# Pairwise outer products with batch norm: other pieces for the stores of rows 38 to 31, and the last sample stored through GpSimd's queue

## The chip, the core and the metric

The kernel runs on one core of one Trainium2 chip. The metric is the device time of one execution in microseconds. A core has five engines with an instruction stream each: TensorE (PE in the profile), VectorE (DVE), ScalarE (ACT), GpSimd (POOL) and SyncE (SP). Data moves between the device's memory and the on-chip memory (128 partitions) by 16 DMA engines; a transfer is issued by an instruction of SP, ACT or POOL into a queue of that engine, and every queue is worked off by the same 16 DMA engines.

## What is computed

For 1024 samples there are two inputs of 39 features with 16 numbers each. For every pair of features (r, c) with c < r, 741 pairs in all, the kernel forms the 16 x 16 outer product of one feature of `xj` and one of `xi`, normalises it by the mean and variance of that pair over the whole batch, and multiplies it by a 16 x 16 weight:

```python
_ROWS, _COLS = np.tril_indices(F1, k=-1)          # 741 pairs, F1 = 39
cross = xj[:, rows, :, None] * xi[:, cols, None, :]
mean = jnp.mean(cross, axis=(0, 2, 3), keepdims=True)
var = jnp.mean(jnp.square(cross - mean), axis=(0, 2, 3), keepdims=True)
normed = (cross - mean) * jax.lax.rsqrt(var + BN_EPS)
normed = normed * gamma[None, :, None, None] + beta[None, :, None, None]
out = normed[:, :, None, :, :] * W[None, None, :, :, :]
return jnp.transpose(out, (0, 2, 1, 3, 4))
```

The output has the shape (1024, 1, 741, 16, 16) in float32: 777 MB, against 6 MB that are read.

## The kernel before

**Tiles.** A partition holds 8 samples (`NT = 8`), so 128 partitions hold all 1024. A *row* r is the set of its r pairs (r, 0) to (r, r-1). One tile is one row for two neighbouring samples (`T = 2`) of every partition, so each row has four tiles, for t0 = 0, 2, 4, 6. The list `tiles` (lines 69 to 76) starts with row 19 (four tiles), then row 20 and its partner 18 in turns, then row 38 (four tiles, no partner), then 37 with its partner 1, 36 with 2, and so on down to 21 with 17. A row and its partner have 38 pairs together; they share a half of the big buffer `y_sb`, and the two halves are used in turns. So a tile writes to the place of the tile two such pairs earlier, and its first instructions have to wait until the stores of that earlier tile have read it. The very last tile of the list is row 17 with t0 = 6.

**The work of one tile.** A batch statistic is folded into a scale and a shift for each pair beforehand (lines 301 to 507). Then, tile by tile (loop at line 523):

- `scale_xi` (POOL, line 169) multiplies the features of `xi` by the scale of each pair, two tiles ahead.
- `products` (lines 177 to 203) makes the outer products: one instruction per sample t and per i of 16, each over all r pairs of a row. In rows above 33 ScalarE does 11 of 16 and GpSimd 5 (`POOL_I_LONG`); else 12 and 4 (`POOL_I`). Sample 0's come first, then sample 1's. Rows up to 4 are done on VectorE (line 192).
- `finish` (lines 254 to 299) adds the shift and multiplies by the weight, pair by pair and for both samples at once: `stt` on VectorE (line 291). A share of the pairs goes to GpSimd: in rows above 33 (`LONG`) eight pairs just ahead of the middle, p0 to p1 with p1 = r // 2, for which ScalarE adds the shift (line 275) and GpSimd multiplies by the weight in two lots of four (line 280); in the other rows 13% of the pairs, at the end of the row, with the shift on GpSimd too (line 277). ScalarE's additions for one tile come ahead of the next tile's products in its stream.
- After each piece that `bounds` names, `finish` calls `store`.

**Pieces and stores.** `bounds(n)` cuts the pairs of a tile into pieces. The first eight tiles have hand-written ones; of the others, rows above 30 (`ONE`) have two equal pieces, the rest one. `store` (lines 205 to 219) issues on SP's queue. In a tile from number 8 on (`whole`) of a row above 19 it stores sample 0 piece by piece and sample 1 as a whole, when the last piece is done. So row 38 has three stores per tile: pairs 0 to 18 of sample 0, pairs 19 to 37 of sample 0, and all 38 pairs of sample 1. Rows 30 to 20 have two, one per sample. A partner row (up to 19) goes out in one store with both samples.

SP works through its stores in order; each waits for the engines that made its piece. Everything is scheduled by hand (`manual_schedule`): the order in which the instructions are written is each engine's order.

Of the kernel before, what the change touches and what calls it, by code (L numbers as in the profile page):

```python
# [14 lines left out]
T = 2  # L15

ONE, LONG = 30, 33
FIRST_PIECES = (  # L20
    (0, 1, 3, 6, 10, 14, 19), (0, 4, 9, 14, 19), (0, 4, 11, 19), (0, 9, 19), (0, 10, 20), (0, 9, 18), (0, 10, 20), (0, 9, 18)
)
# [18 lines left out]
def tile_pair_outer_batchnorm(  # L41
# [15 lines left out]
    nc = tc.nc  # L57
    P = nc.NUM_PARTITIONS
    NB, F, E = xi.shape
    NT = NB // P  # L60
    EE = E * E
# [7 lines left out]
    tiles = [(mid, t0, t0 // T * half // 2) for t0 in range(0, NT, T)]  # L69
# [25 lines left out]
    out_v = out.rearrange("(p t) o n i j -> p t (o n i j)", t=NT)  # L95
# [41 lines left out]
    def view(n):  # L137
        r, _, u = tiles[n]
        return y_sb[:, u : u + T * r, :].rearrange("p (t n) e -> p t n e", t=T)
# [65 lines left out]
    def store(n, c0, c1, t_from=0, t_to=T):  # L205
        r, t0, _ = tiles[n]
        n0 = first[r]

        whole = n >= len(FIRST_PIECES)
        step = 1 if r > mid and (whole or c1 == r) else t_to - t_from  # L210
        for t in range(t_from, t_to, step):
            if whole and step == 1 and t == t_to - 1:
                if c1 < r:
                    continue
                c0 = 0
            nc.sync.dma_start(  # L216
                out_v[:, t0 + t : t0 + t + step, (n0 + c0) * EE : (n0 + c1) * EE],
                view(n)[:, t : t + step, c0:c1, :].rearrange("p t n e -> p t (n e)"),
            )
# [14 lines left out]
    def weigh(n):  # L234

        y = view(n)
        for c0, c1 in zip(bounds(n), bounds(n)[1:]):
            affine(n, range(c0, min(c1, OWN)), (nc.vector,))
            nc.vector.tensor_tensor(  # L239
                y[:, :, c0:c1, :],  # L240
                y[:, :, c0:c1, :],
                w_dve.unsqueeze(1).to_broadcast([P, T, c1 - c0, EE]),
                ALU.mult,
            )
            store(n, c0, c1)

    def bounds(n):
        if n < len(FIRST_PIECES):
            return FIRST_PIECES[n]
        r = tiles[n][0]  # L250
        pieces = 1 + (r > ONE)
        return tuple(q * r // pieces for q in range(pieces + 1))

    def finish(n):

# [32 lines left out]
        for t in range(0, T, size):  # L288
            for c0, c1 in zip(bounds(n), bounds(n)[1:]):
                for c in [*range(c0, min(c1, p0)), *range(max(c0, p1), c1)]:  # L290
                    stt(  # L291
                        y[:, t : t + size, c, :],
                        y[:, t : t + size, c, :],
                        t_sb[:, n0 + c : n0 + c + 1],
                        w_dve.to_broadcast([P, size, EE]),
                        ALU.add,
                        ALU.mult,
                    )
                store(n, c0, c1, t, t + size)
# [262 lines left out]
```

## Time and profile before

| what | value |
|---|---|
| median of 4 runs | 1879.22 us (1879.03 to 1879.45) |
| the profiled execution's own time | 1879.06 us |
| its span, first to last instruction | 1877.3 us |
| VectorE busy | 1723.7 us (92%), 2640 instructions |
| ScalarE busy | 1645.8 us (88%), 3416 instructions |
| GpSimd busy | 1532.3 us (82%), 1746 instructions |
| TensorE busy | 26.0 us (1%) |
| read from, written to the device's memory | 6.00 MB, 776.99 MB |
| one pair on VectorE for two samples (line 291) | 737 ns on average (a little below 0.66 us without a gap in the rows looked at) |
| ScalarE waits for stores in its products (line 147) | 150.4 us, 81 times, longest 4.4 us |

The profile is that of one execution. "Busy" leaves out waiting, and instructions that only issue a transfer. The page gives the span in 40 slices of 47 us with the busy share in tenths (9 is 90% or more) and what the DMA engines moved in GB/s. It also lists groups of instructions by line, with the tile that they write on the left of the arrow and the tiles that they read on the right. In a line of the timeline the first two numbers are the start and the length of a run of instructions in us, then come engine, line, operation, tiles, shapes and the count; in brackets stands how long the engine had been idle before it and what ended that. A trace also holds a record of each DMA packet, with its queue, start, length and size; which of the 16 DMA engines moved it isn't recorded, but packets of one engine follow each other without a gap of more than some ns, so that they can be chained.

### The profile page before, as it was taken

To read this page: it belongs to the slowest core of one execution; us is meant where nothing else is said; L and a number is where in the kernel's file an instruction comes from. 1 tells how busy PE (TensorE), PEld (TensorE's weight loads), DVE (VectorE), ACT (ScalarE), POOL (GpSimd) and SP (SyncE) were. 2 spreads that over 40 slices of the span, in tenths; PEclk is the share of its full clock that TensorE was granted. 3 is DMA by queue.
4 is the path that set the end of the run, shared out by engine and by line. 5 is a ranking of instruction groups with operands and counts; after the bars stand their busy time and mean duration, and the time that the engine had idled before them with its cause. 6 is when DMAs were issued, how large, how long until landed. Compare 5 with 4: busy or idle time off the path is not lost.

```text
span 1877.3 us, 9638 instructions
## 1 busy us (share of the span) xinstructions
PE 26.0 (1%) x130; PEld 23.3 (1%) x130; DVE 1723.7 (92%) x2640; ACT 1645.8 (88%) x3416; POOL 1532.3 (82%) x1746
## 2 busy tenths in 40 slices
PE   4000000000000000000000000000000000000000
PEld 4000000000000000000000000000000000000000
DVE  8999888899999999999999999999999999999994
ACT  8999888888888899989999999998999998989892
POOL 8999778787777788888888888888888888888882
DMA  5999999999999999999999999999999999999998
GB/s 200 386 420 424 411 423 420 429 425 424 428 426 425 428 426 426 427 425 427 419 425 432 425 425 432 425 432 423 431 425 430 425 431 426 429 428 426 428 429 351
DMA packets 53690, 783.63 MB, mean 417 GB/s; under 512 B 4720, under 2 KB 6384, under 8 KB 17008
## 3 DMA queue, kind: packets, MB, share of 16 engines
q1 hardware_dynamic: 52320, 779.72, 97.9%
q10 hardware_dynamic: 1296, 3.29, 0.5%
q14 instruction: 73, 0.60, 0.1%
q8 instruction: 1, 0.02, 0.0%
HBM read 6.00 MB, written 776.99 MB: 417 GB/s over the span
## 4 chain that ended last, share of the span: by engine, by line
DMA 40%; ACT 12%; DVE 6%; issue 1%; SPq 0%; POOL 0%; ACTq 0%; DVEq 0%; POOLq 0%
DMA out_dram<-y_sb 40%; ACT y_sb L147 12%; DVE y_sb L291 6%; SPq L216 0%; POOL y_sb L277 0%; ACTq L147 0%; DVEq L557 0%; DVEq L291 0%; POOLq L277 0%
## 5 line engine op out<-in xcount | busy, mean ns | idle before, releaser
L291 DVE SCALAR_TENSOR_TENSOR y_sb<-y_sb,st_sb,w_dve 128x512 f32<-128x512 f32 (+1 forms) x2511 | 1653.1, 737 | 117.4 <-issue 104.0
L147 ACT ACTIVATE y_sb<-xs,xj_sb 128x288 f32<-128x288 f32 (+20 forms) x3194 | 1514.8, 567 | 181.3 <-DMA out_dram<-y_sb 150.4
L149 POOL TENSOR_SCALAR y_sb<-xs,xj_sb 128x480 f32<-128x480 f32 (+27 forms) x1126 | 604.7, 561 | 14.1 <-DMA out_dram<-y_sb 14.0
L280 POOL TENSOR_TENSOR y_sb<-y_sb,w_sb 128x2048 f32<-128x2048 f32 (+3 forms) x155 | 517.7, 3346 | 87.5 <-ACT y_sb L275 77.9
L169 POOL TENSOR_TENSOR xs<-xi_sb,st_sb 128x640 f32<-128x640 f32 (+33 forms) x135 | 183.9, 1362 | 199.9 <-ACT y_sb L147 196.1
L277 POOL TENSOR_SCALAR y_sb<-y_sb,st_sb 128x512 f32<-128x512 f32 x291 | 196.8, 692 | 5.1 <-ACT y_sb L147 5.1
L275 ACT ACTIVATE y_sb<-y_sb,st_sb 128x512 f32<-128x512 f32 x160 | 100.2, 708 | 3.9 <-POOL y_sb L149 2.2
L192 DVE TENSOR_TENSOR y_sb<-xs,ps 128x256 f32<-128x256 f32 (+3 forms) x32 | 24.8, 817 | 0.5
L489 PE MATMUL ps<-y_sb 39*128 39x38 f32 (+37 forms) x76 | 16.4, 397 | 2.8 <-DVE y_sb L475 2.8
L489 PEld LDWEIGHTS ps<-y_sb 39*128 39x128 f32 x76 | 16.3, 329 | 3.1 <-DVE y_sb L475 3.1
L353 ACT ACTIVATE y_sb<-y_sb 128x1248 f32<-128x1248 f32 x8 | 9.9, 1244 | 2.8 <-POOL y_sb L342 2.8
L358 DVE TENSOR_REDUCE y_sb<-y_sb 128x78 f32<-128x1248 f32 x8 | 11.2, 1445 | 0.4 <-ACT y_sb L353 0.4
L147 ACT ACTIVATE y_sb<-xi_sb,xj_sb 128x304 f32<-128x304 f32 x24 | 11.4, 537 | 0.0
L342 POOL TENSOR_TENSOR y_sb<-xi_sb,y_sb 128x1248 f32<-128x1248 f32 x4 | 9.2, 2320 | 2.2 <-ACT y_sb L391 2.2
L239 DVE TENSOR_TENSOR y_sb<-y_sb,w_dve 128x2048 f32<-128x2048 f32 (+4 forms) x6 | 10.7, 1839 | 0.1
L332 DVE TENSOR_REDUCE y_sb<-xi_sb 128x39 f32<-128x624 f32 (+1 forms) x6 | 6.1, 1011 | 3.9 <-DMA xi_sb<-in_r_xi_dram 3.9
L342 POOL TENSOR_TENSOR y_sb<-xj_sb,y_sb 128x1248 f32<-128x1248 f32 x4 | 9.2, 2321 | 0.0
L378 PE MATMUL ps<-y_sb 128*39 128x79 f32 x48 | 8.1, 340 | 15.2 <-DVE y_sb L358 15.0
L232 POOL TENSOR_SCALAR y_sb<-y_sb,st_sb 128x512 f32<-128x512 f32 x8 | 6.4, 813 | 2.1 <-ACT y_sb L147 2.1
L230 ACT ACTIVATE y_sb<-y_sb,st_sb 128x512 f32<-128x512 f32 x9 | 6.5, 805 | 0.2 <-ACT y_sb L147 0.2
L332 DVE TENSOR_REDUCE y_sb<-xj_sb 128x39 f32<-128x624 f32 (+1 forms) x6 | 6.1, 1013 | 0.6 <-DMA xj_sb<-in_r_xj_dram 0.5
L378 PEld LDWEIGHTS ps<-y_sb 128*39 128x39 f32 x48 | 5.8, 177 | 17.2 <-DVE y_sb L358 10.6
(59 smaller groups left out, 37.3 us busy)
## 6 DMA issues: line engine op xcount, KB each, us to landing
out_dram<-y_sb SPq DMA_DIRECT2D x25, 2304.0 KB, 10.4
out_dram<-y_sb SPq DMA_DIRECT2D x12, 3840.0 KB, 21.6
out_dram<-y_sb SPq DMA_DIRECT2D x21, 2048.0 KB, 12.5
out_dram<-y_sb SPq DMA_DIRECT2D x12, 3584.0 KB, 23.1
out_dram<-y_sb SPq DMA_DIRECT2D x12, 3328.0 KB, 24.4
out_dram<-y_sb SPq DMA_DIRECT2D x12, 3072.0 KB, 25.2
out_dram<-y_sb SPq DMA_DIRECT2D x16, 2176.0 KB, 11.0
out_dram<-y_sb SPq DMA_DIRECT2D x8, 4352.0 KB, 24.1
```

Of the source, the lines that this page charges most:

```text
L147: nc.scalar.activation(y, src, AF.Copy, scale=scale)
L149: engine.tensor_scalar(y, src, scale, 1.0, ALU.mult, ALU.mult)
L169: nc.gpsimd.tensor_tensor(xs, xi_sb[:, t0 : t0 + T, 0:r, :], s_sb[:, :, n0 : n0 + r, :].to_broadcast([P, T, r, E]), ALU.mult,)
L192: nc.vector.tensor_tensor(view(n)[:, t].rearrange("p n (i j) -> p n i j", j=E), xs[:, t].unsqueeze(2).to_broadcast([P, r, E, E]), xj_short ...
L275: nc.scalar.activation(y[:, :, c, :], y[:, :, c, :], AF.Identity, bias=t_c)
L277: nc.gpsimd.tensor_scalar(y[:, :, c, :], y[:, :, c, :], t_c, 1.0, ALU.add, ALU.mult)
L280: nc.gpsimd.tensor_tensor(y[:, :, c0:c1, :], y[:, :, c0:c1, :], w_sb.unsqueeze(1).to_broadcast([P, T, c1 - c0, EE]), ALU.mult,)
L291: stt(y[:, t : t + size, c, :], y[:, t : t + size, c, :], t_sb[:, n0 + c : n0 + c + 1], w_dve.to_broadcast([P, size, EE]), ALU.add, ALU.mult,)
L332: nc.vector.tensor_reduce(total[:, t0:t1, part(x)], sources[x][:, t0:t1], AX.X, ALU.add)
L342: nc.gpsimd.tensor_tensor(devs[n % 7], sources[x][:, t0 : t0 + T], shift[:, x : x + 1, :].unsqueeze(3).to_broadcast([P, T, F, E]), ALU.sub ...
L378: nc.tensor.matmul(ps_g[acc][0:F, 0 : 2 * F + 1], lhs, fb[:, t], start=t == 0, stop=t == NT - 1)
L489: nc.tensor.matmul(ps[:, :, first[r] - n0 : first[r] - n0 + r], pick[:, r, :], stq[:, :, 0:r], start=True, stop=True,)
```

## The change

Three edits. `bounds` gives rows 36 to 31 a first piece of 19, 20, 21, 22, 23, 24 pairs in place of 18, 17, 17, 16, 16, 15; rows 38 and 37 keep 19 and 18. In `store`, `whole` no longer holds for rows 38 and 37, so that their first piece goes out as one store with both samples, and their second piece as one store for each sample: three stores as before, cut differently. And the last tile of all (row 17, t0 = 6), which was one store of both samples on SP's queue, becomes four: sample 0 on SP, then sample 1 as partitions 121 to 125 and 0 to 120 on GpSimd's queue and partitions 126 and 127 on SP's.

```diff
-ONE, LONG = 30, 33
+ONE, LONG, WHOLE = 30, 33, 36
...
     def store(n, c0, c1, t_from=0, t_to=T):
         r, t0, _ = tiles[n]
         n0 = first[r]
-
-        whole = n >= len(FIRST_PIECES)
+        if n == len(tiles) - 1 and t_to - t_from == T:
+
+            store(n, c0, c1, 0, T - 1)
+            for engine, p0, p1 in ((nc.gpsimd, 121, 126), (nc.gpsimd, 0, 121), (nc.sync, 126, P)):
+                engine.dma_start(
+                    out_v[p0:p1, t0 + T - 1, (n0 + c0) * EE : (n0 + c1) * EE],
+                    view(n)[p0:p1, T - 1, c0:c1, :].rearrange("p n e -> p (n e)"),
+                )
+            return
+
+        whole = n >= len(FIRST_PIECES) and r <= WHOLE
         step = 1 if r > mid and (whole or c1 == r) else t_to - t_from
         for t in range(t_from, t_to, step):
             if whole and step == 1 and t == t_to - 1:
...
         if n < len(FIRST_PIECES):
             return FIRST_PIECES[n]
         r = tiles[n][0]
-        pieces = 1 + (r > ONE)
-        return tuple(q * r // pieces for q in range(pieces + 1))
+        if r <= ONE:
+            return 0, r
+
+        return 0, r // 2 + max(0, (WHOLE + 1 - r) * 3 // 2), r
```

## The prediction

> **What bounds the kernel now.** I read the page's slices and DMA queues first.
>
> ```profile
> DMA  5999999999999999999999999999999999999998
> GB/s 200 386 420 424 411 423 420 429 425 424 428 426 425 428 426 426 427 425 427 419 425 432 425 425 432 425 432 423 431 425 430 425 431 426 429 428 426 428 429 351
> q1 hardware_dynamic: 52320, 779.72, 97.9%
> ```
>
> From the second slice on the 16 DMA engines are full; nearly all bytes are stores on SP's queue. 777 MB at about 428 GB/s is 1815 us of the 1877.3 us span. So only three things move the time: stretches in which DMA engines idle, the start, and the end. Slices of 47 us hide such stretches, so next I asked for the busy time in short windows around the rows that change (columns: stretch, length, PE, PEld, DVE, ACT, POOL busy, clock, DMA share, GB/s).
>
> ```profile
> 190.80:193.10 2.30, 0.00 (x0) 0.00 (x0) 1.49 (x3) 2.30 (x5) 0.78 (x2) 1.00 0.00 0
> 239.50:240.30 0.80, 0.00 (x0) 0.00 (x0) 0.00 (x0) 0.80 (x3) 0.00 (x0) 1.00 0.59 243
> 309.70:310.00 0.30, 0.00 (x0) 0.00 (x0) 0.30 (x2) 0.30 (x1) 0.30 (x1) 1.00 0.01 0
> 935.50:936.20 0.70, 0.00 (x0) 0.00 (x0) 0.70 (x2) 0.70 (x3) 0.70 (x2) 1.00 0.30 123
> ```
>
> All engines stand still at 190.8, most or all at 239.5 and 309.7. Chaining the DMA packet records into 16 engines gives the idle time per engine: about 2.35, 0.75 and 0.45 us. At 935.5 (row 30) twelve idle and four work; the same four will matter at the end. The SP timeline shows why 190.8 is empty: the first half of sample 0 of row 38 is issued at 184.13, the rest at 192.32, but the half lasts only 5.8 us (185.05 to 190.85).
>
> ```profile
> 184.13 0.33 SPq L216 DMA_DIRECT2D out_dram<-y_sb  x1
> 192.32 0.81 SPq L216 DMA_DIRECT2D out_dram<-y_sb  x2
> 231.23 0.33 SPq L216 DMA_DIRECT2D out_dram<-y_sb  x1
> 239.40 0.81 SPq L216 DMA_DIRECT2D out_dram<-y_sb  x2
> ```
>
> Next the instruction timeline of the tile two later, (38, t0=4), which reuses that buffer: its 22 products wait for the stores, 11 for sample 0's and 11 for sample 1's, and VectorE waits for the products.
>
> ```profile
> 199.63 7.73 ACT L147 ACTIVATE y_sb<-xs,xj_sb 128x608 f32<-128x608 f32 x11 [0.52 <-DMA out_dram<-y_sb]
> 211.72 7.73 ACT L147 ACTIVATE y_sb<-xs,xj_sb 128x608 f32<-128x608 f32 x11 [4.37 <-DMA out_dram<-y_sb]
> 219.54 19.84 DVE L291 SCALAR_TENSOR_TENSOR y_sb<-y_sb,st_sb,w_dve 128x512 f32<-128x512 f32 x30 [5.92 <-issue]
> ```
>
> Last the DMA view of the end, 1849 to 1877 in 40 slices of 0.7 us.
>
> ```profile
> DMA  9997999989789999989999999982221111100000
> GB/s 474 418 394 332 424 492 461 492 369 430 338 369 471 471 415 490 440 354 459 434 404 404 404 423 448 448 348 100 99 99 75 75 75 75 50 25 25 25 0 0
> ```
>
> One engine moves about 26 GB/s. So at 1868 twelve engines stop, and then four, three, two, one are left: by the packet records they end at 1870.3, 1872.3, 1873.6 and 1876.0, the other twelve at 1867.8 to 1868.2. Queue 14 (instruction fetch) explains it: 62 packets of 8 KB after 27 us, 0.31 us each and some waiting. The four delays, 8.1, 5.6, 4.3 and 2.3 us over the median landing, rank as the instruction counts of ACT (3693), DVE (2935), POOL (2070) and SP (672) do. Each stream seems to be fetched through one DMA engine of its own; TensorE (138) would have a fifth, with next to no delay. The kernel ends when the engine with ACT's fetches is done.
>
> **The change part by part. Rows 38 and 37.** The stores stay three per tile; the first now carries half of both samples. It covers what follows: from 185.05 it lasts 2 x 5.8 = 11.6 us, to 196.65, beyond 192.32 + 0.9 (192.32 to first data at 193.2 is the start of a store). The price: sample 0 now ends as third of four quarters, so its buffer comes free later. Followed through: data of tile (38,0) ends at 202.45 (sample 0) and 208.25 (sample 1) instead of 198.95 and 210.6. The products of (38,4) can start 0.6 after, at 203.05 (3.4 us later than before), run 7.73 to 210.8, then sample 1's to 218.5; the wait of 4.37 is gone, ScalarE itself now sets VectorE's start, 218.6 against 219.54. Its first store is issued 11.7 later (219.54 to 231.23), at 230.3, and could move at 231.2; the queue is full to 208.25 + 4 x 5.8 = 231.45. No idle, 0.25 us to spare. Tile (38,6): products from 226.2, VectorE at 241.7 (242.51 before), data possible at 254.3, queue full to 254.65. Row 37's first tile: VectorE at 264.6 (265.89), data possible at 277.3, queue full to 277.85. Then the margin grows, as products take 7.57 instead of 7.73. So the three stretches go: 2.35 + 0.75 + 0.45 = 3.5 us per engine. On the engine with ACT's fetches it is less, as it lags and idles less in them: some two fetches lie between 185 and 310 (one per 58 us), 0.3 to 0.6 us. I take 2.9. Ends: 3.5, and nothing if ScalarE's start slips by more than the 0.25 us to spare; each us of slip in these tiles comes back as idle.
>
> Does VectorE, while it weighs the second half, have to wait for the two-sample store? No: at 90 to 100 us, where such stores go out piece by piece (ready at 89.23, 93.75, 99.76), it is busy all 10.00 us.
>
> ```profile
> 90.00:100.00 10.00, 0.00 (x0) 0.00 (x0) 10.00 (x16) 10.00 (x23) 9.83 (x13) 1.00 1.00 419
> ```
>
> **Rows 36 to 31.** First pieces grow by 1, 3, 4, 6, 7, 9 pairs. In rows 36 to 34 the piece waits for POOL's share, ready 11.7 us after VectorE's start, while VectorE's 11 to 13 pairs take at most 13 x 0.66 = 8.6: no delay. In rows 33, 32, 31 the first store is issued 6, 7, 9 x 0.66 = 4.0, 4.6, 5.9 us later. What hides it is the queue: bytes issued less bytes moved at that issue are 5.9 to 7.2, 6.5 to 7.0, 7.3 to 8.0 us of work at 428 GB/s. That leaves 1.4 us or more, above the 0.9 of a start. Cost 0. If the lead of 2.9 us were not matched by earlier issues, idle would come back, at most that lead. It is matched: ScalarE waits some 2 us per tile for the previous stores here, so earlier landings start it earlier. Row 30's idle at 935.5 stays; the late engine has none.
>
> **The end.** Before, the last store gives each engine 16 rows of 17 KB (8 partitions, two samples), 0.648 us a row. After, sample 0 still gives 8; sample 1 goes as 5 and 121 partitions on POOL's queue and 2 on SP's. No store of this trace comes from POOL or has such a count. Every store here is split into equal shares of whole rows (128 as 16 x 8). Equal shares of 121 are 11 x 11, of 5 are 5 x 1, and 11 + 5 is 16. So five engines have 1 or 2 rows instead of 8, eleven have 11. If the late engine is one of the five: 6 or 7 rows less, -3.9 or -4.5; take -4.2. If it is one of the eleven: +3 x 0.648 = +1.9. Five streams are fetched and five engines are relieved, so I take the first. The other twelve then end at 1868.1 - 3.5 + 1.9 = 1866.5, before the late one's 1876.0 - 2.9 - 4.2 = 1868.9; a row split small (1 KB packets take 46 ns, 17 of them 0.78 us) adds 11 x 0.13 = 1.5 and stays under it. POOL's issue: between SP's 0.38 us and POOL's longest instruction here, 4.5 us, each; 9 us for both. When it becomes due the queue holds 8.7 us and sample 0 adds 5.2, so it is hidden, and nothing stands behind it on POOL. Two more semaphore waits at the end, 0.06 each: +0.1.
>
> [...]
>
> **Sum.** 1879.06 (this execution; span 1877.3, 1.8 around it; the median shown is 1879.22, 0.16 above) - 2.9 + 0 - 4.2 + 0.1 = 1872.1; I say 1872.0.
>
> **Rivals.** (1) The tail misses: ACT's fetches lie on one of the eleven, or the rows spread evenly. For it: nothing here numbers the engines. Against: the five and five. -2.9 + 1.9 + 0.1 gives 1878.2; spread evenly (0) 1876.3. (2) The middle fails, as the later landing of sample 0 puts ScalarE on the path for more than 0.25 us: only the end gains, 1879.06 - 4.1 = 1875.0. For it the 3.4 us later start, against it the worked margins. (3) Slower: POOL's 121 rows aren't spread. An engine has room until the old end for (1876.0 - (1868.1 - 3.5 - 8 x 0.648)) / 0.648 = 26 rows; from there it decides. 121 has only 1 and 11 as shares, so the price is one engine with 121 rows: 78 us from 1859.4, an end near 1940. Against it: no store in the trace sits on one engine. (4) The change does nothing that counts: the late engine's wait is not what the packets suggest and the removed idle time reappears elsewhere: 1879.
>
> **How the numbers follow.** Forecast 0.56, (1) 0.25, (2) 0.08, (3) 0.06, (4) 0.05. A measurement can tell about 0.2%, 3.8 us: faster means under 1875.5. The forecast and a part of (2) lie there: 0.62; (1), the rest of (2) and (4) but for a little are the same: 0.28; slower 0.10, (3) and part of (1) with a failed middle. Range: below, 3.5 and 4.5 with a little over give 1870.0; above, it takes in (1) at 1878.2: 1878.3.
>
> **What would show it.** Right: no empty window between 185 and 310, (38,4)'s VectorE start near 218.6; a last slice sequence in which no single engine runs on for 8 us, most ending near 1866.5. Wrong: an idle window at first stores of rows 33 to 31; a tail of 25 GB/s as long as before or longer; POOL's packets on few engines.

## The result, and the profile after

The changed kernel takes 1882.34 us (median of 34 runs, 1881.62 to 1883.81) against 1879.19 us (52 runs): the ratio is 1.0018, with a 95% interval of 1.0013 to 1.0023. It is slower by 3.2 us, where 7 us less had been forecast. The profiled execution took 1881.71 us with a span of 1880.0 us.

The page's slices and queues:

```profile
DMA  5999999999999999999999999999999999999998
GB/s 202 386 422 423 426 427 424 426 424 426 427 427 427 426 425 426 429 426 422 425 426 429 426 430 424 431 424 429 429 424 432 428 425 427 431 426 428 426 429 302
q1 hardware_dynamic: 53220, 777.53, 97.7%
q0 software_dynamic: 176, 2.19, 0.4%
```

The fifth slice, with row 38 in it, now moves 426 GB/s (411 before), and the last one 302 (351 before). GpSimd's queue is q0: 2.19 MB and 0.4% of 16 engines' span; its packets took 125 us together by the packet records, where 126 rows of 0.648 us would be 82.

Then the same windows as before the change, moved by 0.3 us because this execution starts a little earlier (columns: stretch, length, PE, PEld, DVE, ACT, POOL busy, clock, DMA share, GB/s):

```profile
190.50:192.80 2.30, 0.00 (x0) 0.00 (x0) 1.53 (x3) 2.30 (x5) 0.82 (x2) 1.00 1.03 440
239.20:240.00 0.80, 0.00 (x0) 0.00 (x0) 0.00 (x0) 0.80 (x2) 0.00 (x0) 1.00 0.93 389
```

The stretch that moved 0 GB/s now moves 440, and the one at 239 moves 389. The SP timeline has the issues as before, 8.2 us apart, but the first one now carries both samples, and its data move until about 196.5 (196.65 had been worked out):

```profile
183.88 0.38 SPq L225 DMA_DIRECT2D out_dram<-y_sb  x1
192.05 1.63 SPq L225 DMA_DIRECT2D out_dram<-y_sb  x2
```

Row 30's idle stretch now stands at 933 and is about half as long (0.39 us per engine on average by the packet records, 0.72 before; the prediction had it stay):

```profile
933.20:933.70 0.50, 0.00 (x0) 0.00 (x0) 0.50 (x2) 0.50 (x2) 0.50 (x2) 1.00 0.29 115
```

Then the timeline of the tile (38, t0=4), whose times had been worked out ahead:

```profile
203.01 15.34 ACT L147 ACTIVATE y_sb<-xs,xj_sb 128x608 f32<-128x608 f32 x22 [4.18 <-DMA out_dram<-y_sb]
218.44 19.84 DVE L302 SCALAR_TENSOR_TENSOR y_sb<-y_sb,st_sb,w_dve 128x512 f32<-128x512 f32 x30 [5.11 <-issue]
226.62 15.35 ACT L147 ACTIVATE y_sb<-xs,xj_sb 128x608 f32<-128x608 f32 x22 [3.17 <-DMA out_dram<-y_sb]
```

The 22 products run without a wait between the samples, from 203.01 (worked out: 203.05), and VectorE starts at 218.44 (218.6); the next tile's products start at 226.62 (226.2). The row part does what the prediction said. So does the lead at the end: sample 0 of the last tile is issued at 1847.88, where the last store was issued at 1850.43 before.

The loss is behind that point. The DMA view of 1846 to 1880 us, in 40 slices of 0.85 us, and the queues in it:

```profile
DMA  9999999999988999699998967776543221100000
GB/s 416 395 421 425 400 405 379 451 395 324 276 219 194 301 296 292 251 424 358 358 271 292 337 184 255 271 276 230 214 164 128 102 123 61 61 20 20 41 0 0
q1 hardware_dynamic: 374, 6.33, 49.7%
q0 software_dynamic: 176, 2.19, 23.0%
out_dram<-y_sb SPq DMA_DIRECT2D x1, 2176.0 KB, 30.6
out_dram<-y_sb POOLq DMA_DIRECT2D x1, 2057.0 KB, 24.2
```

GpSimd's 2 MB took 24.2 us from issue to landing, and sample 0's store on SP 30.6. The timeline of GpSimd shows that its issues were not late, and two windows show what is:

```profile
1848.38 1.28 POOL L212 DMA_DIRECT2D out_dram<-y_sb  x2 [6.75 <-DVE y_sb L302]
```

```profile
1850.00:1852.50 2.50, 0.00 (x0) 0.00 (x0) 0.00 (x0) 0.00 (x0) 0.00 (x0) 1.00 1.00 413
1854.00:1864.00 10.00, 0.00 (x0) 0.00 (x0) 0.00 (x0) 0.00 (x0) 0.00 (x0) 1.00 0.98 291
```

From 1854 on the DMA engines are as busy as before (share 0.98), yet move 291 GB/s instead of 413. GpSimd's first row starts at 1852.77. Busy engines that move less mean that the packets themselves take longer: by the packet records GpSimd's 126 rows of 17 KB took 988 ns on average and up to 3119 ns, where a row of that size took 653 ns (median) before.

Chaining the packet records shows which engine ends last. Four engines lag here as before. In the table a lag is told by the landing of row 17's next to last tile (t0 = 4):

| engine | kernel | lands that tile | rows of 17 KB in the last tile | lost to longer rows | ends |
|---|---|---|---|---|---|
| lags most | rows alone | 1851.67 | 16 | about 0 | 1874.68 |
| lags most | changed | 1850.88 | 8 + 9 = 17 | 1.6 us | 1876.12 |
| lags second | rows alone | 1848.96 | 16 | about 0 | 1872.03 |
| lags second | changed | 1848.36 | 8 + 9 + 1 = 18 | 6.4 us | 1879.10 |

("Rows alone" is the first experiment below. 8 rows are sample 0's on SP's queue, 9 come from GpSimd's queue, 1 from SP's store of two partitions.) So the last engine is no longer the one that lagged most, which is the one with ACT's fetches by the prediction's ranking. The engine that lagged second overtakes it.

### The profile page after: what moved, and what is told of

It reads as the page before. It is cut to its first block, busy times and chain, and to the rows that moved or that the text cites. A ratio compares the mean times of both kernels' runs of the same rounds, so it can differ in the third digit from the quotient of the medians.

```text
span 1880.0 us, 9644 instructions
## 1 busy us (share of the span) xinstructions
PE 26.0 (1%) x130; PEld 23.3 (1%) x130; DVE 1723.7 (92%) x2640; ACT 1645.5 (88%) x3416; POOL 1533.4 (82%) x1748
## 3 DMA queue, kind: packets, MB, share of 16 engines
q0 software_dynamic: 176, 2.19, 0.4%
## 4 chain that ended last, share of the span: by engine, by line
DMA 37%; ACT 13%; DVE 6%; issue 1%; POOL 0%; SPq 0%; ACTq 0%; DVEq 0%; POOLq 0%
DMA out_dram<-y_sb 37%; ACT y_sb L147 13%; DVE y_sb L302 6%; POOL y_sb L288 0%; POOL xs L169 0%; SPq L225 0%; ACTq L147 0%; POOL out_dram L212 0%; DVEq L568 0%; POOLq L568 0%; DVE st_sb L518 0%; DVE ps L511 0%; DVE st_sb L517 0%; DVEq L302 0%; POOLq L212 0%
## 6 DMA issues: line engine op xcount, KB each, us to landing
out_dram<-y_sb SPq DMA_DIRECT2D x16, 2816.0 KB, 24.2
```

## The experiments

Theories at the start: M, two queues at work on the same DMA engines slow each other; S, only the number of rows that each DMA engine gets counts; R, the row changes cost time somewhere. Later P, a row takes longer when an engine reads other partitions than in a store of all 128, and N, a second store at the end costs time, whatever its cut.

**Rows alone, last tile alone, and one store of 128 partitions on another queue.** The first kernel leaves out the special case for the last tile, the second has nothing else. In the third and fourth sample 1 of the last tile is one store:

```diff
-            for engine, p0, p1 in ((nc.gpsimd, 121, 126), (nc.gpsimd, 0, 121), (nc.sync, 126, P)):
+            for engine, p0, p1 in ((nc.gpsimd, 0, P),):      # e4: nc.scalar
```

> The changes to rows 38 to 31 without the change of the last tile. Theory M (two queues at work on the same DMA engines slow each other, so the whole loss lies in the last tile) and theory S (the loss is in how many rows of the last sample each DMA engine gets) both expect 1876.6 us: 1879.2 less the 2.6 us by which the late engine's landings were ahead before the last tile (1853.4 before, 1850.9 after). Theory R (the row changes cost time somewhere) expects 1879 us or more.

> The last tile's change alone, rows as before. M and S: 1879.2 + (1882.3 - 1876.6) = 1884.9 us. R: 1880 us or less.

> As the changed kernel, but sample 1 of the last tile goes in one store of all 128 partitions on GpSimd's queue. S: every engine has its 8 rows again, so 1876.6 us with the end as with one queue. M: rows of two queues still alternate on each engine, the engines move some 280 GB/s instead of 430 while both are live, so 1880 us or more.

> As the changed kernel, but sample 1 of the last tile goes in one store of all 128 partitions on ScalarE's queue. If any second queue slows the engines (M), about the time of the run with GpSimd's queue, 1880 us or more. If the slowing belongs to GpSimd's queue alone (theory G), 1876.6 us. S: 1876.6 us too.

| kernel | us | ratio to before (95%) |
|---|---|---|
| rows alone | 1877.22 | 0.9988 (0.9979 to 0.9997) |
| last tile alone | 1885.55 | 1.0032 (1.0020 to 1.0044) |
| rows, 128 partitions on GpSimd's queue | 1877.48 | 0.9989 (0.9980 to 0.9998) |
| rows, 128 partitions on ScalarE's queue | 1877.16 | 0.9989 (0.9979 to 0.9998) |

The kernel before took 1879.41 us beside them. R falls: the rows alone gain 2.2 us. The last tile alone costs 6.1 us. And M falls: a second queue costs nothing that can be measured, be it GpSimd's or ScalarE's, if the store has all 128 partitions (1877.48 and 1877.16 us against 1877.22). The window of 1854 to 1864 us with GpSimd's 128 rows in it:

```profile
1854.00:1864.00 10.00, 0.00 (x0) 0.00 (x0) 0.00 (x0) 0.00 (x0) 0.00 (x0) 1.00 1.00 426
```

426 GB/s at a share of 1.00, with rows of two queues in turns; GpSimd's 128 rows took 646 to 664 ns each. So it is the cut across the partitions, through the number of rows for each engine (S) or through the length of a row, which S can't explain (988 ns).

**Equal shares, one queue, another cut.** Two stores of 64 partitions on SP's queue give each engine 4 + 4 rows. As a control, two stores of all 128 partitions, of 9 and 8 of the 17 pairs.

```diff
+            for engine, p0, p1 in ((nc.sync, 0, 64), (nc.sync, 64, P)):
...
+            for a, b in ((0, 9), (9, r)):
+                nc.sync.dma_start(
+                    out_v[:, t0 + T - 1, (n0 + a) * EE : (n0 + b) * EE],
+                    view(n)[:, T - 1, a:b, :].rearrange("p n e -> p (n e)"),
+                )
```

> As the changed kernel, but sample 1 of the last tile goes as two stores of 64 partitions on SP's queue: one queue, and 4 + 4 equal rows for each DMA engine. Theory P (a row takes longer when an engine reads partitions other than those that it reads in a store of all 128, since engines then get in each other's way) expects stretched rows, over 0.8 us on average in place of 0.65, and a time of 1879 us or more. Theory S (only the number of rows for each engine counts) expects the time of the kernel with the row changes alone, 1877.2 us, and rows of 0.65 us.

> As the changed kernel, but sample 1 of the last tile goes as two stores of all 128 partitions on SP's queue, 9 and 8 of the 17 pairs. P (the cut across the partitions stretches the rows): rows at the full rate, 1877.2 us. Theory N (a second store at the end costs, whatever its cut): as the two stores of 64 partitions, 1880.6 us.

The halves of the partitions take 1880.57 us (ratio 1.0006, 0.9996 to 1.0016, to a before of 1879.42), the halves of the columns 1877.15 us (0.9991, 0.9982 to 1.0000, to 1879.18). So neither a second store nor GpSimd is needed for a loss of some 3.3 us against the rows alone: the cut across the partitions is enough, at equal shares. Theory S and N fall. The two stretches of 1861 to 1866 us, first the halves of the partitions, then of the columns:

```profile
1861.00:1866.00 5.00, 0.00 (x0) 0.00 (x0) 0.00 (x0) 0.00 (x0) 0.00 (x0) 1.00 1.03 229
```

```profile
1861.00:1866.00 5.00, 0.00 (x0) 0.00 (x0) 0.00 (x0) 0.00 (x0) 0.00 (x0) 1.00 0.91 382
```

All engines are busy in the first, at 229 GB/s, about half of the 426 above. (In the second some are done already, hence 0.91.) The DMA views of 1846 to 1880 us show the whole ends, the rows alone first, then the halves of the partitions:

```profile
DMA  9999999999999899799789823112000000000000
GB/s 411 395 395 446 400 400 430 430 405 405 405 552 388 347 506 445 337 481 496 332 373 594 348 102 143 82 82 102 41 41 41 20 20 0 0 0 0 0 0 0
```

```profile
DMA  9999999999898998999969988966552511000000
GB/s 390 416 420 425 400 425 405 430 405 557 376 470 372 465 465 342 399 312 230 271 189 246 164 246 205 225 164 205 184 164 82 143 61 41 41 20 20 0 0 0
```

With the rows alone twelve engines stop together in slice 24 and the four late ones follow. With the halves the rate falls to 160 to 270 GB/s in slice 19 already, once sample 0's rows run out, and the end is four slices (3.4 us) later.

**GpSimd's two stores by themselves.** They are held back until everything else has landed: GpSimd overwrites one number of sample 0 in each partition of the buffer, which has to wait for SP's store of it (27.22 us of idle time, until 1869.24), and then issues.

```diff
+            nc.gpsimd.memset(view(n)[:, 0, 0:1, 0:1], 0.0)
+            for engine, p0, p1 in ((nc.gpsimd, 0, 121), (nc.gpsimd, 121, 126)):
```

> As the changed kernel, but GpSimd's two stores (121 partitions, then 5) are issued only when sample 0's store has landed: GpSimd first overwrites one number of sample 0 in the buffer, after it was stored. The total is longer by the wait, only the packets count. P: the 121 rows alone, with no second queue, still take well over 0.65 us each, near 1.3 if two engines share; S: 0.65 us. For the shares: 11 rows on eleven engines (as predicted) lasts at least 7.1 us; 8 rows on fifteen engines and one on the last, 5.2 us if unstretched, 10.4 us at 1.3 us a row.

The window of the 121 rows:

```profile
1871.20:1875.20 4.00, 0.00 (x0) 0.00 (x0) 0.00 (x0) 0.00 (x0) 0.00 (x0) 1.00 1.06 226
```

226 GB/s with all engines busy and no other queue. For comparison, the window of the 128 partitions of the next experiment, GpSimd's queue alone too:

```profile
1871.80:1876.30 4.50, 0.00 (x0) 0.00 (x0) 0.00 (x0) 0.00 (x0) 0.97 (x2) 1.00 1.00 405
```

That is 405 GB/s at about the same share. Chained by engine, the packet records give:

```
rows of 17 KB, 126: median 1309 ns, 86 of them over 1200 ns, 19 under 700 ns
121 partitions: 8 rows on each of 15 engines, 1 row on the last
5 partitions:   1 row more on each of 5 engines
```

1309 ns is twice the 653 of the kernel before, as 226 GB/s is about half of 426: a 17 KB row in 1309 ns is 13.3 GB/s, in 653 ns 26.7. Of the 19 rows under 700 ns, 11 start between 1876.5 and 1877.4 us, when most engines are halfway through their eight rows; that is one trace. A cut across the partitions can change which partitions the engines read at the same time, and also which output rows they write; no run separates the reading from the writing. That the cut doubles the time of a row is shown, why it does is not.

**Does GpSimd's queue move on over the engines?** After SP's stores have landed, GpSimd stores 128 partitions x 14 pairs, and three times 5 partitions x 3 pairs.

```diff
+                (nc.gpsimd, 0, P, 0, 14),
+                (nc.gpsimd, 0, 5, 14, 17), (nc.gpsimd, 5, 10, 14, 17), (nc.gpsimd, 10, 15, 14, 17),
```

> When all SP stores have landed, GpSimd's queue stores 128 partitions x 14 pairs of the last sample, and then three times 5 partitions x 3 pairs (SP has stored the other partitions' 3 pairs). If a cursor moves on over the engines, 15 engines get one short row each; if not, five engines get three each and the other eleven none. The 128 rows of 14 KB should take 0.54 us each under every theory.

It doesn't. Five engines get three short rows each, eleven none; the end of two engines of the first kind and one of the second, by the chained packet records (start us, row KB):

```
engine a: 1875.75 14 | 1876.45 3 | 1876.65 3 | 1876.78 3
engine b: 1875.71 14 | 1876.27 3 | 1876.73 3 | 1876.85 3
engine c: 1875.74 14 | done 1876.28
```

The 128 rows took 549 ns (median), near the 539 of a 14 KB row in the kernel before. The second and third short rows took 121 ns each, 25 GB/s an engine, so not every store of a few partitions is slow. SP's single partition, stored ahead of them in this kernel, lands 0.24 us after the median of the store before it, so the engine that gets a single partition is not a late one.

**The same cut on SP's queue alone.**

> As the changed kernel, but the 5 and the 121 partitions go on SP's queue too. If the shares were 11 rows on eleven engines and the late engine among them, it gets 8 + 11 + 1 + 1 rows in place of 16: 1877.2 + 5 x 0.65 = 1880.5 us, more if rows stretch (P). If the late engine isn't among them, below 1877.2 us. If the loss needs GpSimd's queue, 1877.2 us.

A single run: 1883.56 us. Here the shares are those of the prediction: by the landings the 121 partitions run on eleven engines, and in 1864 to 1868 us the DMA share is 0.71, some eleven engines. The 5 partitions land at 1863.56, 1865.94, 1867.78, 1871.30 and 1873.05: one on time and four late, in the steps of the four late engines. So the late engines are among the five, as the edit would have needed. But the program ends 6 us later than with the rows alone: the late engines aren't relieved, neither here nor on GpSimd's queue, where by the chained records four of the five are the late ones too and have 9 rows each.

**The two row changes apart.** Halves for rows 38 and 37 with the old pieces, and growing pieces with the old stores.

```diff
-        whole = n >= len(FIRST_PIECES)
+        whole = n >= len(FIRST_PIECES) and r <= WHOLE
```

> Rows 38 and 37 in halves of both samples alone; first pieces of rows 36 to 31 and the last tile as before. If the growing pieces do nothing (as the prediction had it): 1877.2 us, as the two row changes together. If they give part of the gain: between 1877.2 and 1879.4.

> Growing first pieces of rows 36 to 31 alone. If they do nothing: 1879.4 us, and the idle stretches at 190.8 and 239.5 us stay. If they cost, above it.

Halves alone: 1877.43 us (0.9991, 0.9982 to 1.0000, before 1879.18). Growing alone: 1879.25 us (1.0000, 0.9992 to 1.0009). The gain comes from the halves; the growing pieces alone do nothing that can be measured. In the growing kernel the old hole is still there:

```profile
190.00:193.30 3.30, 0.00 (x0) 0.00 (x0) 2.80 (x5) 3.30 (x6) 2.09 (x3) 1.00 0.26 112
```

The packet records show a small effect of each kind: with halves alone the engines idle 0.46 us on average at row 36 (401.8 us), with both changes 0.12; and the growing pieces bring 0.25 at row 31 (863.5). The two are of similar size and opposite sign.

The kernel with both row changes and the old last tile (1877.2 us) is as fast as halves alone (1877.4) within the noise; either can be kept.

## Why the prediction was wrong

**Rows 38 and 37: right, the size a little off.** The mechanism, the three idle stretches and the tile times came as worked out. The term was -2.9 us; the runs give -2.2 (rows alone) and -1.75 (halves alone, with an interval of the size of the difference). In the changed kernel the latest landing of row 17's next to last tile came 2.6 us earlier than before, 1850.9 against 1853.4, in the kernel of the rows alone 1.8. By the packet records the three stretches held 2.3, 0.7 and 0.3 us per engine on average, 3.3 in all, where 3.5 had been put. Part of the rest is lost to the new small idle stretches (0.08, 0.08 and 0.12 us on average at 255, 302 and 402 us); why the two profiles differ by 0.8 us stays open.

**Rows 36 to 31: right.** Costed at nothing, measured 1.0000 (0.9992 to 1.0009, so some 1.6 us either way). The queue hid the later issue, but barely: the 1.4 us left at row 31 let some engines idle up to 0.5 us; the late ones, which set the end, didn't.

**The end: two steps failed.** The first: "Equal shares of 121 are 11 x 11, of 5 are 5 x 1, and 11 + 5 is 16." GpSimd's queue gave 8 rows to fifteen engines and 1 to the last, and where it stored 5 partitions three times in a row, all three went to the same five engines. No engine was relieved, and no run shows the term of -4.2: on GpSimd's queue the late engines had more rows, not fewer, and on SP's queue, where 121 partitions did run on eleven engines, the program ended 6 us later than with the rows alone (1883.56 us, a single run). The four late ones got 9 rows of GpSimd's in place of 8, and the one that lagged second got one of SP's two as well: SP's store of 2 partitions landed at 1871.72 and 1879.10, and the second is the last landing of the program. On the engine that lags most that is 17 rows for 16, +0.65 us where -4.2 stood; on the next one 18, +1.3.

The second step was the price of a row, 0.648 us, with 0.78 as the upper bound, from rows that all belonged to stores of 128 partitions. In a store of 121, rows took 1.31 us alone and 0.99 us in the changed kernel. The forecast bounded the price by the size of packets and never by the cut across the partitions. This is the larger part: at equal shares the cut alone costs 3.3 us (1880.57 against 1877.22, each beside its own before), of some 5.3 that the last tile costs in the changed kernel (+3.15 against -2.19 to before). In the changed kernel the packet records account for the last engine: 1872.03 with the rows alone, less 0.6 of earlier start, plus 1.3 for two rows, plus 6.4 for longer rows gives 1879.1, its landing. So it passes the engine that lags most, which lost only 1.6 us to longer rows. That this engine ends the kernel, which the prediction took over from before, no longer held.

**The rivals.** The first, "the tail misses", had the right place and the wrong price: with even shares it gave 1876.3, as it left rows at full rate. The third, unspread rows, didn't come. What would have been needed was a rival for the row itself: slower packets with engines that stay busy. The cover for GpSimd's issue held (both stores issued within 1.3 us). The +0.1 for two more semaphore waits doesn't show: the program ends 0.90 us after the last landing in both kernels.

**Instruction fetch.** The trace before has 73 fetch packets of 8 KB after 27 us, not 62. At 0.31 us each they make 22.6 us, against 20.3 for the four delays together. So fetch fits as the reason for the delays, beside the ranking by instruction counts; that each stream has one DMA engine of its own was not shown.

## What to carry to other kernels

When DMA engines bound a kernel, look for windows in which they move nothing: here a store that was shorter than the wait for the next one, cured by storing half of both samples first. Cut a store by columns and keep all 128 partitions: that cut cost nothing here, while stores of 64 partitions on SP's queue and of 121 on GpSimd's ran at half rate (229 and 226 GB/s). Before moving work between DMA engines by the number of partitions, measure which engines a queue really uses, with a small store issued after all else has landed.

## What the runs showed of the hardware

- A store of a part of the partitions can run at half rate with all 16 engines busy: 226 GB/s against 426, rows of 1309 ns against 653 for 121 partitions, 229 GB/s for halves. A high DMA share is no proof of a high rate.
- Two queues at once cost nothing that could be measured: 426 GB/s with rows of SP's and GpSimd's queues in turns, 1877.48 us against 1877.22.
- GpSimd's queue spread 121 partitions as 8 rows on fifteen engines and 1 on the last, and gave three stores of 5 partitions in a row to the same five engines; on SP's queue 121 partitions ran on eleven engines.
- Four DMA engines end this kernel late, by 2.3 to 8.1 us over 1877 us; in the unchanged kernel that sets its end. The delays rank as the instruction counts of four engines do, which fits instruction fetch (73 packets of 0.31 us). The four are among the five engines that SP's store of 5 partitions used.
